# A transformer layer in one kernel: the last tiles' scales apart, more look-ahead at the end of the list, and slack behind the rounding of the feed-forward weights

## The chip, the cores and the metric

The kernel runs on one core of a Trainium2 chip. The metric is the device time of one execution in microseconds. The core has five engines that take their own instruction queues in order: PE (TensorE; its weight loads are shown as PEld), DVE (VectorE), ACT (ScalarE), POOL (GpSimd) and SP (SyncE), which here only issues transfers.

## The reference

One pre-norm transformer layer over an input of 2 sequences of 2048 tokens, 256 wide: causal attention of 16 heads of 16 with rotary positions, and a gated feed-forward layer of 704 whose activations and weights are rounded to FP4 in blocks of 16.

```python
x = x + attn(layernorm(x))           # softmax(q k^T / 4, causal) v, then Wo
x = x + ffn(layernorm(x))

def fp4_quant_dequant(x):            # blocks of 16 along the last dimension
    scale = maximum(max(abs(xb)) / 6, 1e-12)
    return GRID[searchsorted(MID, abs(xb / scale))] * sign(xb) * scale

def fp4_linear(x, w):
    return einsum('bsk,nk->bsn', fp4_quant_dequant(x), fp4_quant_dequant(w))

h = silu(fp4_linear(x, w_gate)) * fp4_linear(x, w_up)
return fp4_linear(h, w_down)
```

## The kernel before

**Work.** A sequence is four chunks of 512 tokens, a chunk four tiles of 128. The eight chunks are counted 0 to 7 here (`order`), and tile 6.3 is the last tile of chunk 6. For each chunk the kernel normalizes and projects (`norm_steps`, `project_steps`), takes the row maxima of the scores for four groups of four heads (`max_steps`; scores L1064, reduced on DVE at L1088), computes the scores again with keys on the partitions, takes exponentials on ACT and multiplies with the values (`value_steps`; L1196, L1204, L1219, L1252), divides, and runs the feed-forward layer tile by tile (`ffn_steps`). The feed-forward weights come in 18 parts (`load_rounded`): load, round, transpose on PE (L656), copy.

**A tile of the feed-forward layer.** Load `x0` and add the bias on POOL (L1472); output projection `po` (L1488), added to `x0` on DVE (L1502); statistics on DVE, the power on POOL (L520, L521); normalize (L530); round; transpose (`pth`, L1403); gate and up products in two halves each (`pg`, L1543) with DVE's L1572 and L1577; round `h`; transpose; down product `pd` (L1636, six blocks in two tasks), added on DVE (L1645) and stored (L1648). The last chunk's four tiles, 7.0 to 7.3, use space that attention has left: `own` lies in a `qT` buffer, so a load of `x0` into it has to wait until a group of heads has read its queries. They also divide by way of a transposition (L1347) and round `h` on DVE (`ON_VECTOR`); all other tiles round `h` on POOL.

**Rounding** (`fp4`): DVE finds the block scales and their reciprocals (L554 to L558), POOL shrinks the reciprocals a little (L562), POOL or DVE multiplies (L565), DVE makes a power of two of each element (L581, L584), and POOL or DVE adds and subtracts it (L587, L590) and multiplies the scale back (L593). Scale and reciprocal lie in rotating pairs of small tiles: the kinds `sc16` (256 columns) and `sc44` (704 columns).

**The list.** Nothing is issued in the order of the source. Each step becomes a task with an engine, a cost in us, a due time, and the things that it reads and writes (`Plan.add`). `Plan.ordered` plays the tasks through with the costs and writes the list: at each turn it takes, over all engines, the task that can start first; among those of one engine that could start within `PATIENCE` of each other, the one due first. For PE a change of the array's shape (64-row strips for scores, 128 by 32 for values, whole for the rest) counts `CHANGE` on the due time. It looks only at tasks due within `AHEAD` = 3 of the earliest one still open. Buffers are rooms (`ROOM`); a task that needs one waits for all users of an older thing. `late` is time that the list adds before users on other engines may start. The engines then follow the list as it is written; the chip's own waits decide when.

Due times are in units of the attention's work: a group of heads of chunk c is c + 1 units, all of it 80, so one unit is about 16 us. The last chunk's tiles are due from the end of attention on. Those of chunk 6 are spread up to four units past the end of attention (`LATE`), so that 6.3 is left over among the last tiles.

```python
horizon = dues[-1][0] + AHEAD                                   # Plan.ordered
...
return due + (CHANGE if e == PE and t.tiling != tiling else 0.0)   # rank
...
add(SP, landing(128), run, [rows_[b, c]] if last else [], [things["x0"]], due)   # ffn_steps.load
```

The last of these lines makes the load of a last tile's `x0` a reader of `rows_`, which the last division writes.

Of the kernel before, what the change touches and what calls it, by code (L numbers as in the profile page):

```python
# [29 lines left out]
F32 = mybir.dt.float32  # L30
# [8 lines left out]
P = 128  # L39
# [26 lines left out]


AHEAD = 3
CHANGE = 0.07
FEED_M = 0.0  # L70
FEED_V = 0.0
PATIENCE = 0.03
TURN = 0.3
ISSUE = 0.46

SLACK = 6.0

# [13 lines left out]
ROOM = dict(ps=7, av=1, ex=4, qT=4, parts=4)  # L91
ROOM.update(mx=2, mparts=1, left=1, mT=2, avs=1, den=2, y=2, sums=2, over=1)
ROOM.update(xnT=1, xin=XIN, high=1, t1=1, t2=1, cs=1, dev=XIN-1)
ROOM.update(x0=1, xT=1, x1=2, xn=2, h=1, hrT=1, step=1, fdev=2, sc16=2, sc44=2)


ANY_TURN = ("ps",)
# [31 lines left out]
class Plan:  # L129
# [3 lines left out]
    def __init__(self):  # L133
        self.tasks = []
        self.made = {}

    def add(
        self, engine, cost, run, reads=(), writes=(), due=0.0, books=(), tiling="whole", feeds=0.0,
# [38 lines left out]
    def ordered(self):  # L177

        waiting = {e: [] for e in HOP}
        for n, t in enumerate(self.tasks):  # L180
            if not t.left:
                waiting[t.engine].append((t.due, n, t))
        number = {t: n for n, t in enumerate(self.tasks)}
        free = dict.fromkeys(HOP, 0.0)
        rooms = {kind: [] for kind in ROOM}
        turn = dict.fromkeys(ROOM, 0)
        tiling = "whole"
        dues = sorted(((t.due, n) for n, t in enumerate(self.tasks)), reverse=True)
        done = set()
        out = []  # L190

        def vacancy(kind, n, to):

            held = rooms[kind]
            n -= ROOM[kind] - len(held)
            if n <= 0:
                return 0.0, []
            some = []
            for thing in held:
                if all(u.end is not None for u in thing.users):  # L200
                    at = max(
                        u.end + (u.late if u.engine != SP else 0.0) + HOP[u.engine][to]
                        for u in thing.users
                    )
                    some.append((at, thing.number, thing))
            if len(some) < n:
                return None
            some = sorted(some)[:n]
            return some[-1][0], [thing for *_, thing in some]

        while len(out) < len(self.tasks):
            while dues and dues[-1][1] in done:
                dues.pop()
            horizon = dues[-1][0] + AHEAD
            choice = None
            for e, queue in waiting.items():
                queue.sort(key=lambda x: x[:2])
                able = []
                vacant = {}
                for due, n, t in queue:  # L220
                    if due > horizon or len(able) > 30:
                        break
                    at = max(t.ready, free[e])
                    for kind, some in t.kinds.items():
                        if kind not in ANY_TURN and some[0].number != turn[kind]:
                            break
                        key = kind, len(some)
                        if key not in vacant:
                            vacant[key] = vacancy(*key, e)
                        if vacant[key] is None:  # L230
                            break
                        at = max(at, vacant[key][0])
                    else:
                        able.append((at, due, n, t))
                if not able:
                    continue
                first = min(at for at, *_ in able)
                if choice and first > choice[0] + 1e-9:
                    continue

                def rank(x):
                    at, due, n, t = x
                    return due + (CHANGE if e == PE and t.tiling != tiling else 0.0)

                pick = min((x for x in able if x[0] <= first + PATIENCE), key=rank)
                if choice is None or pick[0] < choice[0]:
                    choice = pick
            at, due, n, t = choice
            e = t.engine
            waiting[e].remove((due, n, t))  # L250
            for kind, some in t.kinds.items():
                for thing in vacancy(kind, len(some), e)[1]:
                    rooms[kind].remove(thing)
                rooms[kind] += some
                turn[kind] += len(some)
            if e == PE:
                if t.tiling != tiling:
                    at += ENTER[t.tiling]
                tiling = t.tiling
            if e == SP:  # L260
                free[e] = at + ISSUE * t.late
                t.end = free[e] + t.cost
            else:
                t.end = free[e] = at + t.cost
            done.add(n)
            out.append(t)
            for a in t.after:
                a.left -= 1
                late = t.late if a.engine != e and e != SP else 0.0
                a.ready = max(a.ready, t.end + late + HOP[e][a.engine])  # L270
                if not a.left:
                    waiting[a.engine].append((a.due, number[a], a))
        self.span = max(t.end for t in out)
        return out
# [29 lines left out]
def layer_kernel(  # L304
# [226 lines left out]

        add(DVE, 0.33, run, *things, due)

    def fp4(src, thing, r, n, engine=POOL, step_of=None):

        nb = n // BLOCK
        st = {}
        small16 = Thing("sc16" if nb <= 16 else "sc44")
        queue = nc.gpsimd if engine == POOL else nc.vector
        plain = on_pool(n) if engine == POOL else on_vector(n)  # L540
        by_block = 0.14 + 1.71e-3 * n if engine == POOL else on_vector(n)
# [6 lines left out]

        def scaled(due):
            def sizes():  # L550
                scale = ffn.tile([P, nb], F32, tag=f"scale{n}", name="scale")[:r]
                inv = ffn.tile([P, nb], F32, tag=f"inv{n}", name="inv")[:r]
                st["scale"], st["inv"] = scale, inv
                nc.vector.tensor_reduce(  # L554
                    scale, blocks(src()), AX.X, ALU.max, apply_absolute_value=True
                )
                nc.vector.tensor_scalar(scale, scale, 1.0 / 6.0, 1e-12, ALU.mult, ALU.max)
                nc.vector.reciprocal(inv, scale)  # L558

            def nudged():  # L560
                inv = st["inv"]
                nc.gpsimd.tensor_scalar(inv, inv, NUDGE, 1.0, ALU.mult, ALU.mult)  # L562

            def divided():
                queue.tensor_tensor(blocks(src()), blocks(src()), spread(st["inv"]), ALU.mult)  # L565

            add(DVE, on_vector(n) + 0.36 + 0.005 * nb, sizes, [thing], [small16], due)
            add(POOL, 0.17, nudged, [small16], [small16], due)
            add(engine, by_block, divided, [small16], [thing], due)

        def rounded(due):
# [24 lines left out]
            add(DVE, 0.263 + 1.033e-3 * n, powers, [thing], [step], due)  # L596
            add(engine, plain, added, [step], [thing], due)
            add(engine, plain, taken, [step], [thing], due)
            add(engine, by_block, scaled_back, [small16], [thing], due)

        return scaled, rounded

# [33 lines left out]
    def load_rounded(w, row, rows, col, cols, put, target):  # L636

        st = {}
        raw = Thing("xn")
        scaled, rounded = fp4(lambda: st["raw"], raw, rows, cols)  # L640

        def load(due):
            def run():
# [779 lines left out]
    def ffn_steps(b, c, i, last=False):  # L1423
# [33 lines left out]
        def load(due):  # L1457
            def run():
                token("x0")
                nc.sync.dma_start(st["x0"], x[b, t * P : (t + 1) * P, :])  # L1460

            add(SP, landing(128), run, [rows_[b, c]] if last else [], [things["x0"]], due)

        def turn_attended(due):
            def put():
# [43 lines left out]
        def scaled(due):  # L1509
            def dst():  # L1510
                token("xn")
                return st["xn"]

            got, dev = st["by"]
            normed(
                dst, lambda: st["x1"], got, ([dev, things["x1"]], [things["xn"]]), due
            )

            def step_of():

                things["x0"].tile = lambda: st["x0"]
                return things["x0"]

            first, st["rounded"] = fp4(
                lambda: st["xn"], things["xn"], P, E, step_of=step_of if last else None
            )
            first(due)

# [65 lines left out]
        def scaled_gated(due):  # L1594
            def step_of():
                step = Thing("ex")
                step.tile = lambda: wide("step")
                return step

            first, st["rounded"] = fp4(  # L1600
                lambda: st["hf"],
                things["h"],
                P,
                I,
                DVE if last and i in ON_VECTOR else POOL,
                step_of if last else None,
            )
            first(due)

# [253 lines left out]
    begun += [(-8.5 + 0.1 * n, step) for n, step in enumerate(both)]  # L1863
    for at, step in sorted(begun + main + side, key=lambda x: x[0]):
        step(at)
    for t in plan.ordered():
        t.run()
        in_order(t.end < DAWN)
# [62 lines left out]
```

## Time and profile before

| | |
|---|---|
| median of 3 runs | 1390.26 us (1388.22 to 1392.69) |
| the profiled execution | 1384.36 us, of which the span is 1382.6 |
| mean granted clock | 0.972 |
| PE busy | 1307.6 us (95%) |
| DVE busy | 1106.0 us (80%) |
| ACT, POOL busy | 752.0 (54%), 538.4 (39%) |

Busy time is summed over the span; a wait is idle time of an engine ahead of an instruction, put down to what ended it. In rows of the time line the columns are start, length, engine, line, operation, output and inputs with shapes, count, and in brackets the idle time before and its releaser. Groups of instructions that follow each other are merged in such rows. PE's busy time is modelled, and a PE that is busy need not be at its peak.

### The profile page before, as it was taken

The page shows a single profiled execution, that of the slowest core. Times are in us where ns is not written, and L with a number is a line of the kernel's source. Part 1 is how long each engine was busy: PE and PEld are TensorE (multiplying, and loading weights), DVE is VectorE, ACT ScalarE, POOL GpSimd, SP SyncE. Part 2 cuts the span into 40 slices and gives each one's busy share as a digit, 9 for nine tenths or more (in the row PEclk, how much of TensorE's full clock was granted, in tenths as well). Part 3 has the DMA queues.
Part 4 walks back from the last instruction along what each step waited for, and adds up shares of the span by engine and source line. Part 5 has one row for each costly group of instructions (what it writes and reads, how often), then busy time and mean ns, then how long its engine had stood idle before and what let it go on. Part 6 is the DMA issues. An engine that isn't in the chain of part 4 may idle for free.

```text
span 1382.6 us, 27442 instructions
## 1 busy us (share of the span) xinstructions
PE 1307.6 (95%) x10269; PEld 650.5 (47%) x10269; DVE 1106.0 (80%) x2415; ACT 752.0 (54%) x1670; POOL 538.4 (39%) x685
## 2 busy tenths in 40 slices
PE   6887999999999999999988999999999999999967
PEld 4444444444544444444454555454454444444445
DVE  7788989978889988875467978997879888884286
ACT  3532665556556566558643455455655566668711
POOL 4654735434323434314345544343443232311262
PEclk9976999999999999999999999999999999999989
DMA  2544433411221401211444414240130130000000
GB/s 88 132 130 103 100 89 66 102 35 55 56 46 39 109 22 35 67 32 51 98 107 108 104 30 107 65 97 18 55 82 20 43 81 9 9 6 5 13 9 19
DMA packets 61886, 84.37 MB, mean 61 GB/s; under 512 B 14772, under 2 KB 30520, under 8 KB 61752
## 3 DMA queue, kind: packets, MB, share of 16 engines
q1 hardware_dynamic: 61744, 82.61, 23.7%
q8 instruction: 81, 1.33, 0.4%
q14 instruction: 53, 0.43, 0.1%
q10 hardware_dynamic: 8, 0.00, 0.0%
HBM read 55.09 MB, written 27.49 MB: 60 GB/s over the span
## 4 chain that ended last, share of the span: by engine, by line
PE 62%; DVE 20%; POOL 5%; issue 5%; DMA 5%; ACT 2%; SPq 0%; POOLq 0%; DVEq 0%; ACTq 0%
PE av L1252 14%; DVE parts L1088 9%; PE sc L1064 9%; PE pg L1543 9%; PE sx L1196 8%; PE sx L1204 7%; PE pd L1636 5%; PE pj L808 3%; PE pth L1403 2%; PE po L1488 1%; PE pv L990 1%; DVE scale L554 1%; PE sc L1033 1%; DVE step L581 1%; DVE step L584 1%
## 5 line engine op out<-in xcount | busy, mean ns | idle before, releaser
L1219 ACT ACTIVATE ex<-sx 128x512 f32<-128x512 f32 (+3 forms) x1280 | 593.5, 538 | 345.8 <-PE sx L1204 207.9
L1088 DVE TENSOR_REDUCE parts<-sc 128x1 f32<-128x512 f32 (+3 forms) x1152 | 638.4, 611 | 64.8 <-PE sc L1064 49.2
L1204 PE MATMUL sx<-qT,kT 64*128 64x512 f32 (+3 forms) x1280 | 337.7, 523 | 0.0
L1064 PE MATMUL sc<-kT,qT 64*128 64x512 f32 (+3 forms) x1280 | 290.3, 432 | 12.5 <-DMA kT<-parts 4.2
L1252 PE MATMUL av<-ex,v 128*32 128x512 f32 (+3 forms) x2560 | 300.1, 541 | 0.0
L1196 PE MATMUL sx<-mT,less 64*128 64x512 bf16 (+3 forms) x1280 | 250.7, 356 | 9.3 <-DVE parts L1088 3.4
L1064 PEld LDWEIGHTS sc<-kT,qT 64*128 64x128 f32 x1280 | 139.1, 192 | 176.4 <-DVE parts L1088 55.2
L1196 PEld LDWEIGHTS <-less 64*128 64x128 bf16 x1280 | 68.5, 94 | 212.9 <-issue 205.4
L562 POOL TENSOR_SCALAR inv<-inv 128x16 f32<-128x16 f32 (+2 forms) x82 | 17.7, 216 | 384.8 <-DVE inv L558 362.9
L1204 PEld LDWEIGHTS sx<-qT,kT 64*128 64x128 f32 x1280 | 132.5, 196 | 13.0 <-issue 10.6
L1636 PE MATMUL pd<-wdT,hrT 128*128 128x256 f32 (+1 forms) x384 | 100.9, 402 | 2.0 <-ACT hrT L1407 1.4
L1252 PEld LDWEIGHTS av<-ex,v 128*32 128x32 f32 x2560 | 51.7, 108 | 69.8 <-issue 59.8
L860 POOL TENSOR_TENSOR t<-t,cs 128x512 f32<-128x512 f32 x31 | 39.9, 1287 | 106.7 <-DVE t L854 100.4
L1636 PEld LDWEIGHTS pd<-wdT,hrT 128*128 128x128 f32 (+1 forms) x384 | 68.1, 191 | 27.2 <-issue 13.6
L1088 DVE TENSOR_REDUCE mx<-sc 128x1 f32<-128x128 f32 (+3 forms) x128 | 54.6, 478 | 31.2 <-PE sc L1033 31.0
L808 PE MATMUL pj<-xnT,wqkT 128*128 128x512 f32 x128 | 75.3, 685 | 3.3 <-DVE v L999 1.7
L1543 PE MATMUL pg<-wgT,xT 128*128 128x352 f32 x224 | 77.3, 477 | 0.3 <-ACT xT L1407 0.2
L1543 PE MATMUL pg<-wuT,xT 128*128 128x352 f32 x224 | 74.5, 472 | 0.2
L1033 PE MATMUL sc<-pick,mask_q 64*128 64x64 bf16 x1024 | 71.8, 202 | 0.0
L587 POOL TENSOR_TENSOR h<-h,step 128x704 f32<-128x704 f32 x28 | 47.2, 1685 | 57.8 <-DVE step L584 54.5
L1033 PE MATMUL sx<-pick,mask_k 64*128 64x64 bf16 x1024 | 63.5, 197 | 0.0
L1569 ACT ACTIVATE h<-pg 128x352 f32<-128x352 f32 x64 | 29.9, 467 | 56.8 <-PE pg L1543 51.6
(156 smaller groups left out, 1522.3 us busy)
## 6 DMA issues: line engine op xcount, KB each, us to landing
qT<-parts SPq DMA_DIRECT2D x120, 128.0 KB
kT<-parts SPq DMA_DIRECT2D x120, 128.0 KB
parts<-high SPq DMA_DIRECT2D x30, 256.0 KB
parts<-t SPq DMA_DIRECT2D x30, 256.0 KB
sums<-avs SPq DMA_DIRECT2D x28, 256.0 KB
cs<-in_rope_dram SPq DMA_DIRECT2D x8, 512.0 KB
xin<-in_L_attn_x_dram SPq DMA_DIRECT2D x28, 128.0 KB
y<-sums SPq DMA_DIRECT2D x28, 128.0 KB
```

The source lines that it names most:

```text
L587: queue.tensor_tensor(src(), src(), st["step"], ALU.add)
L808: nc.tensor.matmul(got["pj"], lhsT=wqkT[:, k, i, cols], rhs=xnTs[b, c][:, k, :], start=(k == 0), stop=(k == KE - 1),)
L860: (nc.gpsimd if early and i == 0 else queue).tensor_tensor(swapped, swapped, angles[b, c][:, 1, :], ALU.mult)
L1033: nc.tensor.matmul(sc[h][:, col + at : col + at + STRIP], lhsT=strips(mask, h, half), rhs=strips(pick, h), start=False, stop=(half == 1),)
L1064: nc.tensor.matmul(sc[h][:, :cols], lhsT=strips(qT, h, d, slice(i * P, (i + 1) * P)), rhs=strips(kT, h, duo, slice(0, cols)), start=True, ...
L1088: nc.vector.tensor_reduce(dst, got[0][h][:, :cols], AX.X, ALU.max)
L1196: nc.tensor.matmul(sc[h][:, off:], lhsT=strips(less[d], h), rhs=strips(mT, h, slice(off, CH)), start=True, stop=False,)
L1204: nc.tensor.matmul(sc[h][:, off:], lhsT=strips(kT, h, duo, slice(jj, jj + P)), rhs=strips(qT, h, d, slice(off, CH)), start=False, stop=(j ...
L1219: nc.scalar.activation(st[j, d][:, h, off:], got[0][h][:, off:], AF.Exp, scale=HD**-0.5)
L1252: nc.tensor.matmul(st["av"][SLOT * s : SLOT * (s + 1), off:], lhsT=v[:, at : at + SLOT], rhs=st[j, d][:, h, off:], start=(j == 0), stop=(j ...
L1543: nc.tensor.matmul(got[half], lhsT=split("xrT")[:, k, :], rhs=wT[:, k, half * IH : (half + 1) * IH], start=(k == 0), stop=(k == KE - 1),)
L1636: nc.tensor.matmul(st["pd"], lhsT=st["hrT"][:n, k, :], rhs=wdT[:n, k, :], start=(k == 0), stop=(k == KI - 1),)
```

## The change

Five edits. (1) `CHANGE` goes from 0.07 to 0.1. (2) `NEAR`: once the earliest open task is due within eight units of the end of attention, the list looks ahead over everything (50) in place of 3. (3) The last chunk's tiles get scale and reciprocal tiles of their own, the kinds `endsc16` and `endsc44`. (4) Their loads of `x0` no longer wait for the rows of the last division and are due one unit sooner. (5) `EASE`: in the list alone, whoever uses a rounded part of the weights on another engine may start 3 us after the last step of the rounding. No instruction is added, removed or changed in size; the places of the instructions in the five queues change, from the first weight parts on, and the program gets the new small tiles.

```diff
-CHANGE = 0.07
+CHANGE = 0.1
+EASE = 3.0
+NEAR = 8.0
-ROOM.update(... sc16=2, sc44=2)
+ROOM.update(... sc16=2, sc44=2, endsc16=2, endsc44=2)
...
+        self.near_end = None
...
-            horizon = dues[-1][0] + AHEAD
+            horizon = dues[-1][0] + (AHEAD if dues[-1][0] < self.near_end else 50.0)
...
-    def fp4(src, thing, r, n, engine=POOL, step_of=None):
+    def fp4(src, thing, r, n, engine=POOL, step_of=None, end=False, weight=False):
-        small16 = Thing("sc16" if nb <= 16 else "sc44")
+        own = "end" if end else ""
+        small16 = Thing(f"{own}sc16" if nb <= 16 else f"{own}sc44")
...
-                scale = ffn.tile([P, nb], F32, tag=f"scale{n}", name="scale")[:r]
-                inv = ffn.tile([P, nb], F32, tag=f"inv{n}", name="inv")[:r]
+                scale = ffn.tile([P, nb], F32, tag=f"{own}scale{n}", name="scale")[:r]
+                inv = ffn.tile([P, nb], F32, tag=f"{own}inv{n}", name="inv")[:r]
...
-            add(engine, by_block, scaled_back, [small16], [thing], due)
+            add(engine, by_block, scaled_back, [small16], [thing], due, late=EASE * weight)
...
-        scaled, rounded = fp4(lambda: st["raw"], raw, rows, cols)
+        scaled, rounded = fp4(lambda: st["raw"], raw, rows, cols, weight=True)
...
-            add(SP, landing(128), run, [rows_[b, c]] if last else [], [things["x0"]], due)
+            add(SP, landing(128), run, [], [things["x0"]], due - 1.0 * last)
...
+    plan.near_end = end - NEAR
     for t in plan.ordered():
```

In `ffn_steps` both calls of `fp4` pass `end=last`.

More of the change, by code (lines that the diff above doesn't have):

```diff
@@ L93 @@
 ROOM.update(xnT=1, xin=XIN, high=1, t1=1, t2=1, cs=1, dev=XIN-1)
-ROOM.update(x0=1, xT=1, x1=2, xn=2, h=1, hrT=1, step=1, fdev=2, sc16=2, sc44=2)
+ROOM.update(x0=1, xT=1, x1=2, xn=2, h=1, hrT=1, step=1, fdev=2, sc16=2, sc44=2, endsc16=2, endsc44=2)
 ANY_TURN = ("ps",)
@@ L1524, in scaled @@
             first, st["rounded"] = fp4(
-                lambda: st["xn"], things["xn"], P, E, step_of=step_of if last else None
+                lambda: st["xn"], things["xn"], P, E, step_of=step_of if last else None,
+                end=last,
             )
@@ L1606, in scaled_gated @@
                 step_of if last else None,
+                last,
             )
```

## The prediction

> **What bounds the kernel now.** I read the stages first, then the long chain that ended last, then the tail engine by engine. The stage table (length, busy time and count for PE, PEld, DVE, ACT, POOL, then granted clock) has three regimes.
>
> ```profile
> 50.00:100.00 50.00, 42.38 (x388) 24.04 (x380) 35.58 (x94) 21.25 (x56) 30.92 (x44) 0.80 0.54 133
> 100.00:150.00 50.00, 42.03 (x307) 21.25 (x306) 42.88 (x100) 21.34 (x48) 25.50 (x38) 0.73 0.45 112
> ...
> 200.00:1200.00 1000.00, 975.13 (x7770) 476.00 (x7762) 829.67 (x1775) 570.16 (x1249) 381.02 (x443) 1.00 0.24 61
> 1200.00:1300.00 100.00, 99.92 (x828) 42.28 (x826) 60.38 (x121) 71.81 (x153) 20.58 (x24) 1.00 0.02 5
> 1300.00:1383.00 83.00, 63.18 (x324) 40.82 (x322) 53.75 (x110) 18.67 (x54) 29.38 (x46) 0.92 0.05 17
> ```
>
> From 200 to 1300 us PE is busy 97.5 to 99.9%: only a better fit of the list could gain there. Losses lie at the start, while the feed-forward weights are prepared, and in the tail. At the start the weights' transposes (L656) hold PE, which takes its queue in order:
>
> ```profile
> 110.41 0.51 PE L656 MATMUL ptr<-ident,wr 128*128 128x128 f32 x2 [2.22 <-POOL wr L593]
> ...
> 128.83 0.69 PE L656 MATMUL ptr<-ident,wr 128*128 128x128 f32 x2 [4.37 <-POOL wr L593]
> ```
>
> The bracket is PE's idle time ahead of the row: two of four stalls, 8.5 us together. The second has a deeper cause: POOL itself waited 12.93 us for a DVE instruction behind fourteen reductions.
>
> ```profile
> 117.95 7.93 DVE L1088 TENSOR_REDUCE parts<-sc 128x1 f32<-128x512 f32 x14 [1.97 <-PE sc L1064]
> ...
> 126.55 0.72 POOL L587 TENSOR_TENSOR wr<-wr,step 128x256 f32<-128x256 f32 x1 [12.93 <-DVE step L584]
> ```
>
> In the tail (after the last attention product, 1310 us) PE stands still while the last tiles are normalized and rounded:
>
> ```profile
> 1313.23 1.41 POOL L1472 TENSOR_TENSOR own<-own,bob 128x256 f32<-128x256 f32 x2 [17.46 <-DMA own<-in_L_attn_x_dram]
> ...
> 1325.11 0.69 PE L1403 MATMUL pth<-ident,own 128*128 128x128 f32 x2 [9.14 <-POOL own L593]
> 1326.31 4.05 PE L1543 MATMUL pg<-wgT,own 128*128 128x352 f32 x8 [0.52 <-ACT own L1407]
> 1330.20 2.53 PE L1543 MATMUL pg<-wuT,own 128*128 128x352 f32 x8
> ```
>
> and the chain ends through the leftover tile 6.3 (start, length, work):
>
> ```profile
> 1363.36 1.68 POOL h L587
> ...
> 1365.11 1.67 POOL h L590
> ...
> 1367.17 2.10 POOL h L593
> ...
> 1369.31 0.67 PE pth L1403 x4
> ...
> 1370.65 4.48 PE pd L1636 x12
> 1375.13 0.60 PE pth L1403 x4
> ...
> 1376.39 3.07 PE pd L1636 x12
> ```
>
> DVE had finished tile 7.3's rounding at 1372.98 (its last L593 started 1372.09, 0.89 long), but 7.3's transposes started at 1375.06, behind 6.3's down product.
>
> **The change, part by part.** The orders of instructions of the two programs show the moves; durations are rows of the trace.
>
> **Tail** (look-ahead, scales apart, earlier loads; they only work together). In the new order 6.3's normalized tile is rounded before attention ends, where POOL now idles for 17.46 us; its transposes and first gate half stand between the last division's transposes and 7.0's, and its other three halves right after the four output projections, in PE's 9.14 us gap. Step by step:
> - DVE is the full engine from 1333 to 1373: busy 9.79 + 20.41 + 8.43 - 0.84 = 37.8 of 40 us. Of 6.3, two L1572 and two L1577 (0.5 each), the three scale instructions (1.5) and the two of L581 and L584 (1.06) now precede that stretch: 4.6 us. They go where DVE is idle: 1310 to 1333 has 10.93 + 4.19 us of work in 23, so 7.9 free. Gain 4.6.
> - DVE's waits for POOL's L562 at the end (0.78 and 0.38, POOL busy with 6.3) go: 1.2. But for 7.1 and 7.2 scale and division now stand next to each other, with the trip over POOL between (DVE's L558 ended at 1344.86, POOL's 0.23 us began at 1344.95: about 0.35 each way through): 0.7 back. Gain 0.5.
> - 7.3's transposes no longer stand behind 6.3's down product: 1375.06 - 1372.98 = 2.1.
> - The start. The x0 loads (2.44 us in the chain, landed at 1312.3 + 2.4) come early: the new order has the first three before attention's end, the fourth after the last score, about 1306. Against that 6.3's half (1.35) and transposes (0.4) delay 7.0's own by about 1.3. The additions then run at the projections' pace instead of the loads', and POOL's rounding of 7.0 is no longer cut by 6.3's five instructions (0.2 + 0.62 + 0.73 + 0.77 + 0.62 = 2.9). Walking 7.0's chain with these rows puts its transposes at about 1323.4, not 1325.1: 1.7. The first eight gate products took 4.05 against 2.53 for the next eight; PE busy beforehand removes 1.5. As DVE's filling already uses part of this, I count half of 3.2: 1.6.
> - PE will instead be idle some 4 us before 7.3's transposes. The row nearest to that is 6.3's down product, 4.48 after 3.03 + 0.46 us of idling against 3.07 otherwise: 1.4 back.
>
> [...]
>
> Sum of the tail: 4.6 + 0.5 + 2.1 + 1.6 - 1.4 = 7.4, say 7.5. Bounds: DVE's 53.75 us of work after 1310 plus 7.5 for the last transpose, copy, product and store end at 1371 at best, 11 to gain; and 3 if only the late waits go.
>
> Moving 6.3's POOL rounding also moves collisions. In the trace DVE's L581 on 704 columns has a median of 516 ns and a maximum of 1592, DVE's L590 886 and 1639, each time beside POOL's 1.69 us instructions at 1358 to 1369. The same three POOL instructions now meet 7.0's work: I count zero net.
> [...] The trace shows the old place paying already.
>
> **Weights eased by 3 us.** In the new order the transposes behind the 2.22 and 4.37 us stalls have 6 and 10 PE tasks more ahead of them, those behind the other two (0.92, 0.99) 4 and 17, at some 0.8 us a task. If all stalls go: 8.5. But during the longest DVE was reducing without a pause, and PE's extra scores would queue for it; and some weights' rounding moves later on POOL too (the seventh from 61st to 66th place). The last weight's transpose goes from 229th to 250th of 2119 PE tasks, well ahead of the first down product at 306. Between 0 and 8.5 I take 3.
>
> **Cost of changing the array's shape, 0.07 to 0.1.** Meant to save changes of shape, but the order has 1114 of them against 1115. About half of all tasks stand at another place, mostly by one to five. PE's idle time from 200 to 1200 is 24.9 us; a different fit can add or remove some of it. I take 0, with 4 either way.
>
> Total 7.5 + 3 + 0 = 10.5 from the profiled execution's 1384.36: 1373.9, a ratio of 0.9924. The median of the runs shown is 1390.26, so 1379.7, say 1380.
>
> **The rivals.**
> - *The body gives it back (no change).* Tail 3 to 5, weights nothing, order 2 to 4 worse: 1387 to 1390. For it: half the list is moved. Against: the tail is read off directly.
> - *The stalls stay (smaller gain).* POOL's rounding moves with the transposes, PE waits 8.5 us as before: 7.5 alone, 1382.7. For it: the 12.93 us wait on DVE, which no easing mends.
> - *DVE is flooded (slower).* A larger shape cost lets strips of scores run on, DVE's reductions fall behind and PE's loads wait for PSUM. PE's weight loads already wait 55.2 us for L1088, in 90 waits. It decides once that grows by 14.7 us, 27%: then the gains are gone and 4.2 more, 1394 and above. For it: DVE is 96% busy from 400 to 500 us. Against: as many shape changes as before, so runs of one shape are no longer on average.
>
> **How the numbers follow.** Forecast (both gains) 0.55, stalls stay 0.20, no change 0.13, slower 0.12. A measurement of this kernel can tell about 0.3%, 4.2 us, from nothing; so faster 0.75, same 0.13, slower 0.12. The range reaches from both bounds (11 + 8.5 off: 1370) to no gain at all (1390).
>
> **What would show it.** Right: no L1472 waiting for the load; 6.3's L1543 rows before 7.0's; the last L593 on DVE followed at once by 7.3's transposes; 62 to 69 us from the last division's transposes (1310.0 now) to the end, where there are 72.6; PE's L656 stalls under 4 us in sum. Wrong: PE idle time from 200 to 1300 us up by more than 8 us, or DVE idle for more than 6 us after 1333.

## The result and the profile after: slower by 0.72%

The changed kernel takes 1400.34 us, the median of 5 runs (1397.06 to 1401.36); the kernel before took 1389.79 beside it (1387.15 to 1392.69). The ratio is 1.0072, 95% interval 1.0059 to 1.0084. The forecast was 1380 with a range up to 1390: sign and range were both missed. The profiled execution took 1400.52 us, its span is 1398.7.

The stage table of the changed kernel (columns as before):

```profile
50.00:100.00 50.00, 42.80 (x356) 24.91 (x358) 30.71 (x84) 20.19 (x52) 26.26 (x36) 0.73 0.50 120
100.00:150.00 50.00, 42.18 (x312) 22.36 (x312) 39.56 (x103) 18.59 (x46) 23.93 (x37) 0.73 0.46 108
200.00:1200.00 1000.00, 974.99 (x7715) 480.49 (x7714) 831.51 (x1760) 563.83 (x1239) 375.87 (x435) 0.99 0.25 62
1300.00:1399.00 99.00, 83.14 (x448) 48.19 (x446) 61.37 (x120) 34.34 (x85) 34.78 (x50) 0.93 0.03 10
```

In the middle PE is as busy as before (974.99 for 975.13, at a granted clock of 0.99 for 1.00). The first rows carry the loss: in the same 50 us DVE gets 84 instructions done for 94, busy 30.71 us for 35.58. As marks I take the copies of the attended values (`avs`), one for each group of heads. The sixth starts at 203.2 us, 189.7 before; the ninth at 328.6, 315.0 before; the last at 1325.6, 1308.5 before. Some 13 of 17 us are lost in the first 200, while the weights are prepared, and 3.5 between the ninth mark and the last. (The profiled execution of before was a quick one, 5 us under its median; the medians differ by 10.6 us.)

The stalls that EASE was to remove are gone. PE's waits from 25 to 205 us after the change (in all, times, longest) no longer show the 8.5 us for POOL at the weights' transposes, L656 before and L662 now:

```profile
PE ptm L1151 <- DVE mslots L1135: 3.9, 3, 2.4
PE sc L1070 <- DVE parts L1094: 3.8, 3, 3.3
...
PE ptr L662 <- DVE parts L1094: 0.5, 1, 0.5
```

PE now waits for DVE instead, and DVE for something new. Its waits from 20 to 330 us, before:

```profile
DVE scale L554 <- DMA wr<-in_L_ffn_w_gate_dram: 5.9, 2, 3.5
...
DVE scale L554 <- DMA wr<-in_L_ffn_w_up_dram: 1.9, 1, 1.9
```

and after:

```profile
DVE scale L560 <- DMA wr<-in_L_ffn_w_up_dram: 8.7, 2, 6.8
DVE scale L560 <- DMA wr<-in_L_ffn_w_gate_dram: 8.0, 2, 4.8
```

`wr` is the raw part of the weights; with a shorter wait that is not shown, 8.2 us of waiting for its loads became 16.8. The longest wait on DVE's time line, and SP's queue at the same time:

```profile
107.36 0.73 DVE L860 STREAM_SHUFFLE t<-qb 128x512 f32<-128x512 f32 x1
114.92 0.42 DVE L560 TENSOR_REDUCE scale<-wr 128x16 f32<-128x256 f32 x1 [6.83 <-DMA wr<-in_L_ffn_w_up_dram]
```

```profile
105.08 3.66 SPq L930 DMA_DIRECT2D kT<-parts  x8
108.85 0.83 SPq L651 DMA_DIRECT2D wr<-in_L_ffn_w_up_dram  x2
```

Read it backwards. DVE stands at its reduction because the load was issued at 108.85. It was issued then because all the parts share two buffers: a part is loaded into the buffer of the part two before it, which that part's transposes on PE set free. The seventh part's transposes ran at 105.7 us, 83.1 before; the ninth part's load, which needs that buffer, went out at 108.85 (86.85 before), behind the eight transfers of `kT`. EASE puts 3 us into each turn of this ring: from the end of the seventh part's rounding to its transposes it is 5.6 us here (from 100.1) and was 2.6 before (from 80.5). The rest of the 22 us by which the load is later had gathered ahead of that. And the reductions stand in DVE's order where the list took the load to have landed, 2.5 us after its issue; here the reduction came 6 us after it.

The tail, from the last division's transposes (1327.10) to the end, is 71.6 us for 72.6. The chain that ended last:

```profile
1386.60 0.81 DVE h L596
1387.43 0.90 DVE h L599
...
1388.38 1.13 PE pth L1409 x4
...
1390.17 5.42 PE pd L1644 x12
```

7.3's transposes now follow DVE's last step at once, and 6.3 is out of the chain. But the last product takes 5.42 us for 3.07.

### The profile page after: what moved, and what is told of

It reads as the page before. It is cut to its first block, busy times and chain, and to the rows that moved or that the text cites. A ratio compares the mean times of both kernels' runs of the same rounds, so it can differ in the third digit from the quotient of the medians.

```text
span 1398.7 us, 27458 instructions
## 1 busy us (share of the span) xinstructions
PE 1329.5 (95%) x10269; PEld 665.3 (48%) x10269; DVE 1119.1 (80%) x2415; ACT 750.4 (54%) x1670; POOL 537.4 (38%) x685
## 4 chain that ended last, share of the span: by engine, by line
PE 62%; DVE 22%; issue 5%; DMA 5%; POOL 3%; ACT 2%; SPq 0%; POOLq 0%; DVEq 0%; ACTq 0%
PE av L1258 14%; PE sc L1070 9%; DVE parts L1094 9%; PE sx L1202 8%; PE pg L1550 8%; PE sx L1210 7%; PE pd L1644 5%; PE pj L814 2%; PE pth L1409 2%; PE po L1494 2%; DVE step L587 1%; DVE scale L560 1%; DVE mx L1094 1%; PE pv L996 1%; PE sc L1039 1%
## 5 line engine op out<-in xcount | busy, mean ns | idle before, releaser
L1210 PE MATMUL sx<-qT,kT 64*128 64x512 f32 (+3 forms) x1280 | 341.9, 527 | 0.0
L1070 PE MATMUL sc<-kT,qT 64*128 64x512 f32 (+3 forms) x1280 | 293.6, 438 | 16.0 <-DVE parts L1094 5.2
L1202 PE MATMUL sx<-mT,less 64*128 64x512 bf16 (+3 forms) x1280 | 255.3, 358 | 9.5 <-DVE parts L1094 3.6
L1070 PEld LDWEIGHTS sc<-kT,qT 64*128 64x128 f32 x1280 | 142.6, 195 | 164.7 <-DVE parts L1094 52.3
L1644 PE MATMUL pd<-wdT,hrT 128*128 128x256 f32 (+1 forms) x384 | 105.1, 414 | 0.8 <-ACT hrT L1413 0.8
L1258 PEld LDWEIGHTS av<-ex,v 128*32 128x32 f32 x2560 | 52.6, 108 | 71.6 <-issue 61.8
L525 POOL TENSOR_SCALAR ve<-mv 128x1 f32<-128x1 f32 x64 | 12.6, 197 | 140.3 <-DVE mv L521 136.8
```

The lines of the kernel that those rows point to most:

```text
L1070: nc.tensor.matmul(sc[h][:, :cols], lhsT=strips(qT, h, d, slice(i * P, (i + 1) * P)), rhs=strips(kT, h, duo, slice(0, cols)), start=True, ...
L1202: nc.tensor.matmul(sc[h][:, off:], lhsT=strips(less[d], h), rhs=strips(mT, h, slice(off, CH)), start=True, stop=False,)
L1210: nc.tensor.matmul(sc[h][:, off:], lhsT=strips(kT, h, duo, slice(jj, jj + P)), rhs=strips(qT, h, d, slice(off, CH)), start=False, stop=(j ...
L1258: nc.tensor.matmul(st["av"][SLOT * s : SLOT * (s + 1), off:], lhsT=v[:, at : at + SLOT], rhs=st[j, d][:, h, off:], start=(j == 0), stop=(j ...
L1644: nc.tensor.matmul(st["pd"], lhsT=st["hrT"][:n, k, :], rhs=wdT[:n, k, :], start=(k == 0), stop=(k == KI - 1),)
```

## Experiments

DVE's idle times below are sums of the gaps ahead of its instructions from 20 to 330 us in each run's trace; "for loads" is the part ended by a load of `wr`.

| run | ratio to before, 95% | DVE idle | for loads |
|---|---|---|---|
| before | 1 | 45.2 | 8.2 |
| the change | 1.0072 (1.0059 to 1.0084) | 53.5 | 16.8 |
| change_alone | 0.9961 (0.9946 to 0.9977) | 45.3 | 7.9 |
| ease_alone | 1.0087 (1.0069 to 1.0105) | 57.4 | 16.3 |
| tail_alone | 0.9988 (0.9972 to 1.0004) | 50.2 | 8.7 |
| mid_alone | 1.0085 (1.0056 to 1.0114) | 57.4 | 18.8 |
| no_ease | 0.9943 (0.9924 to 0.9961) | 46.8 | 8.3 |
| ease_3rooms | 1.0003 (0.9992 to 1.0015) | 45.9 | 6.2 |
| plain_3rooms | 0.9996 (0.9979 to 1.0013) | 43.2 | 3.6 |
| nudged_list | 1.0026 (1.0014 to 1.0038) | 46.7 | 8.7 |
| nudged_list_2 | 1.0062 (1.0044 to 1.0079) | 53.1 | 8.1 |
| ease_late_landing | 1.0051 (1.0031 to 1.0070) | 53.1 | 0.0 |
| shape_cost_012 | 1.0034 (1.0020 to 1.0047) | 45.0 | 9.0 |
| ease_loads_early | 1.0035 (1.0017 to 1.0053) | 51.1 | 0.0 |
| after_loads_early | 1.0007 (0.9990 to 1.0024) | 46.9 | 0.0 |
| plain_loads_late | 1.0035 (1.0020 to 1.0049) | 53.4 | 13.4 |
| warm_fill | 0.9975 (0.9961 to 0.9988) | 44.6 | 7.8 |
| warm_fill_2 | 0.9926 (0.9905 to 0.9947) | 44.2 | 8.0 |

The idle times come from one execution each, the ratios from all of them, and executions of one list differ. tail_alone has before's list up to about 1190 us, and yet DVE idles 5.0 us more in it and the ninth mark comes 5.3 us later. Its waits for loads are steadier, 8.7 for 8.2.

**Which edit.** The change in its parts, each on the kernel before.

```diff
-CHANGE = 0.07
+CHANGE = 0.1        # change_alone, and with EASE mid_alone
+EASE = 3.0          # ease_alone, on the last step of a weight part's rounding
                     # tail_alone: NEAR, endsc16/endsc44, the x0 loads
```

change_alone. 

> The kernel before with one edit, CHANGE 0.07 to 0.1; the list is the same up to PE's 229th task (about 170 us). Theory A, the loss is made in the first 200 us, by an order in which the array runs at half clock for longer (the changed kernel had lost 13 us by 200 us): this edit then costs little, end of attention within 4 us of 1310, median 1387 to 1394. Theory B, the shape cost makes runs of scores that hold PE for DVE: +8 to +15 us, spread from 200 us on, median 1398 or more.

ease_alone. 

> The kernel before with one edit, EASE 3.0 on the weights' rounding. Theory A: most of the loss is here, 8 to 14 us by 200 us, longer stretches of half clock before 200 us, median 1398 to 1404. Theory B: the stalls on the weights go and nothing else, median 1384 to 1390.

tail_alone. 

> The kernel before with the three edits of the end (look-ahead, scales apart, earlier loads); the list is the same up to PE's 1908th task (about 1190 us). From the changed kernel's trace: 3.8 us earlier at the last transposes, 2.8 given back by an array at half clock behind its 3.4 us of idling. Both theories: end of attention as before within 2 us, tail 69 to 72 us against 72.6, median 1386 to 1391. My recorded sum would be 1382.

mid_alone. 

> The kernel before with CHANGE and EASE and without the three edits of the end. If the losses of the parts simply add, its time less that of the kernel before is the sum of those of the two edits alone, and end of attention is near 1327 (17 later). If the two lists are merely two draws from a wide scatter, it stands apart from the sum by 5 us or more.

EASE alone loses 0.87%, more than the whole change; CHANGE alone gains 0.39%, and with EASE in the list that gain is not to be found (mid_alone, where the two ratios multiplied would be 1.0048). change_alone, at 1385.3 us, is faster than either theory had it. The tail edits are worth 0.12%, 1.7 us, with an interval that still holds nothing; in the profile of tail_alone attention ends 7 us later than before, where both theories said within 2, and the tail is 70.0 us. Without EASE the rest should then be the better kernel.

```diff
-            add(engine, by_block, scaled_back, [small16], [thing], due, late=EASE * weight)
+            add(engine, by_block, scaled_back, [small16], [thing], due)
```

no_ease. 

> The change without EASE: CHANGE 0.1 and the edits around the end. If EASE alone makes the loss and the rest adds up, the ratio to before is 0.9961 x 0.9988 = 0.995, about 1384 us. If CHANGE's gain is luck of one list that any further edit undoes, it is 0.998 to 1.000.

It is: 1384.6 us, as the two ratios multiplied say.

**Why EASE costs.** EASE's list stands as before's ahead of PE's 36th task and behind its 436th (of 2119). I first tried a third buffer, in the list and in the tiles, with EASE and without.

```diff
-ROOM.update(... xn=2 ...)
+ROOM.update(... xn=3 ...)
-... tag="xn", name="wr", bufs=2)
+... tag="xn", name="wr", bufs=3)
```

ease_3rooms. 

> EASE alone (ratio 1.0087 with two rooms) with a third buffer for the raw weight parts, in the list and in the tiles. Theory L: the loss comes from the loads. A part is loaded into the buffer of the part two before it, which its transposes set free; EASE puts those transposes later in PE's order, so the loads stand later in SP's, and DVE's reduction of the next part stands at the head of DVE's queue until the load lands (16.3 us of such idling with EASE, 8.4 us without). With a third buffer that idling falls to 8 us or less and the time to that of the next run, within 0.3%, at or below 1391. Theory R: any other order of the first 320 us costs or gains up to a percent by the phases of the clock and the waits of in-order queues; then the third buffer has no sure effect, and EASE may still lose 0.5% or more against the next run. Theory C (the array's half clock): the loss stays at 8 to 12 us whatever the loads do, with 10 us or more of half clock above before's in the first 200 us.

plain_3rooms. 

> The kernel before with only the third buffer for the raw weight parts: the yardstick of the run before it. Theory L: DVE's idling for these loads falls from 8 us to 3 us or less, and the time by 0 to 6 us, ratio 0.996 to 1.000. Theory R: anything from 0.993 to 1.007.

The waits for loads fall from 16.3 to 6.2 us and the loss from 0.87% to nothing, within 0.3% of the same edit without EASE. That fits late loads; but the third room also moves tasks on every engine. So I asked what a list costs that is only different.

```diff
-WEIGHTS = 8
+WEIGHTS = 8.1       # nudged_list; 8.2 in nudged_list_2
```

nudged_list. 

> The kernel before with one planner constant moved that has nothing to do with the change (WEIGHTS from 8 to 8.1, a due time of the weights' parts): 390 of PE's 2119 tasks stand elsewhere, none before task 56 or after 896. Theory R: it differs from before by 0.4% or more either way, as EASE does. Theory L: it differs by what DVE idles for the loads of the weight parts more or less than before's 8 us, at 1.0 to 1.4 us of time for one of idling, and without a difference there by under 0.3%.

nudged_list_2. 

> As the nudged list (1.0026), with the constant at 8.2: a second sample of what a list costs that is only different. Theory R: beyond 0.4% either way. Theory L: within 0.4%, and DVE idles 6 to 11 us for the loads of the weight parts.

Both are slower, by 0.26 and 0.62%, with before's waits for loads. Theory L expected less than 0.4%, and the second misses that. A nudge of a list costs a few tenths of a per cent here; EASE's 0.87 is above both samples, but not so far that the rest needs no test. The other route to the same end, a longer landing in the list's costs:

```diff
-            add(SP, landing(128), run, [], [raw], due)
+            add(SP, landing(128) + 3.0, run, [], [raw], due)
```

ease_late_landing. 

> EASE alone with two rooms, but in the list's costs the load of a raw weight part takes 3 us longer (5.5 for 2.5, where the traces show 3 to 7 us from issue to the reduction), so that DVE's reduction of it is placed later in DVE's order. Theory L (the loss is DVE held at the head of its queue by a load that the list takes to have landed): DVE's idling for these loads falls from 16.3 us to 9 or less although rooms and EASE are as they were, and the time to within 0.4% of before, 1385 to 1396. Against it: EASE's later transposes cost by themselves, and the ratio stays at 1.007 to 1.011.

The waits for loads go to 0.0 and 40% of the loss goes with them, but DVE idles 53.1 us, of that now 13.6 for the loads of `den` (3.5 before), and the ratio is outside what theory L named. Undecided so far. The next three runs leave PE, DVE, ACT and POOL with the same instructions in the same order and move loads in SP's order only; the first two also have the third buffer.

```diff
+    order = plan.ordered()
+    for k in range(3, len(loads)):      # ease_loads_early, after_loads_early; SOONER = 6.0
+        at = to = order.index(loads[k])
+        first = order.index(turns[k - 3]) + 1
+        while to > first and order[to - 1].end > loads[k].end - landing(128) - SOONER:
+            to -= 1
+        order.insert(to, order.pop(at))
-... tag="xn", name="wr", bufs=2)        # and every other "xn" tile; the list keeps two rooms
+... tag="xn", name="wr", bufs=3)
...
+    for k, n in {9: 2, 10: 2}.items():  # plain_loads_late: behind the next two tasks of SP
+        at = to = order.index(loads[k])
+        while n:
+            to += 1
+            n -= order[to].engine == SP
+        order.insert(to, order.pop(at))
```

ease_loads_early. 

> EASE alone with its list kept on PE, DVE, ACT and POOL instruction for instruction; the raw weight parts get a third buffer, and their loads stand up to 6 us of the list's time earlier in SP's order. Theory L (late loads): DVE's idling for them falls from 16.3 us to 9 or less and the ratio from 1.0087 to 1.000 to 1.004. Theory R (the order of the list itself): the waits go, others take their place, and the ratio stays at 1.006 or above.

after_loads_early. 

> The whole change with the same edit of its loads and nothing else. Theory L: from 1.0072 to 0.996 to 1.001, the tail edits' 0.1 to 0.2% and the rest of EASE's loss in it. Theory R: 1.005 or above.

plain_loads_late. 

> The kernel before with two loads later in SP's order and nothing else moved on any engine: the tenth part's behind one transfer and the eight of kT that EASE's list puts ahead of it (issued at 106 in place of 99.5 us), the eleventh's behind two loads of x. Theory L: DVE meets the tenth part's reduction at about 103 us and now waits some 6 us there; of that the eleventh part's wait of 1.8 us and that for den (2.8 us) right behind may be saved, so 2 to 6 us reach the end: ratio 1.0015 to 1.0045. Theory R: no order but SP's has moved, so within 0.15%.

All three measured what theory L named, and none what theory R named. With its loads early the whole change goes from 1.0072 to 1.0007 and EASE from 1.0087 to 1.0035. Against the change without EASE (no_ease, 0.9943) the early loads give back about half of EASE's cost: 1.0072 is 1.30% above it, 1.0007 still 0.64%. Two loads put back in the kernel before cost 0.35%, 4.9 us. The DVE time line of that run shows the changed kernel's wait remade:

```profile
102.55 0.74 DVE L831 SCALAR_TENSOR_TENSOR t<-pj,bqk,cs 128x512 f32<-128x512 f32 x1
110.22 0.42 DVE L555 TENSOR_REDUCE scale<-wr 128x16 f32<-128x256 f32 x1 [6.93 <-DMA wr<-in_L_ffn_w_up_dram]
```

In the kernel before that reduction started at 101.67 without a wait. The kernel before with its own loads early was not run, so how much it would gain by them too is not known; plain_3rooms, the nearest, gained 0.04% with 3.6 us of waiting for 8.2.

With its loads early EASE has another wait, that for `den`. DVE's waits of ease_loads_early, and the longest of them on the time line:

```profile
DVE den L1333 <- DMA den<-sums: 13.6, 3, 7.0
```

```profile
107.43 0.25 DVE L1333 RECIPROCAL den<-den 128x16 f32<-128x16 f32 x1 [6.96 <-DMA den<-sums]
```

EASE alone has 6.8 us for `den` and before 3.5. SP issues this transfer no later (100.9 us, 107.3 in EASE alone), but DVE, which no raw part holds any more, stands at it from 100.5 on. So in part theory R holds: in these two traces 10 of the 16.3 us of waits that went came back as others. This trace is of an execution of 1401.3 us, where the median is 1394.1; that of after_loads_early, of 1393.0 with a median of 1391.9, has 11.8 us for `den`. That these waits make the rest of EASE's cost is not shown. Three rooms in the list itself (ease_3rooms) keep both small, 6.2 us for the loads and 7.6 for `den`.

**CHANGE.** Was its gain that of saved changes of shape?

```diff
-CHANGE = 0.07
+CHANGE = 0.12
```

shape_cost_012. 

> The kernel before with CHANGE at 0.12 alone: PE's order has 1092 changes of the array's shape, 1115 before and 1102 with CHANGE at 0.1, which measured 0.9961, that is 5.4 us for 13 changes less. If the gain is that of the changes saved, 23 less are worth up to 9.6 us, ratio 0.993; if it was the luck of one list, anything from 0.996 to 1.003.

Slower by 0.34% with the fewest shape changes. A gain by saved changes would have grown; CHANGE at 0.1 was one list among others, and a fortunate one.

**The cold products of the tail.** Fill PE's last two idle stretches, in the change without EASE.

```diff
+    def warm(t, fill, n):               # into a PSUM tile that nobody reads
+        spare = small(CH, "spare")
+        for k in range(fill):
+            j = k % (n // P)
+            nc.tensor.transpose(spare[:, (k % TPC) * P : (k % TPC + 1) * P], t[:, j * P : (j + 1) * P], ident)
...
             def powers():               # tile 7.0: 12; in warm_fill also 7.3: 16
                 ...
+                warm(t, fill, n)
             def taken():                # in warm_fill_2, 7.3: 16
+                warm(st["step"], late_fill, n)
```

warm_fill. 

> The change without EASE (1384.6 us), and PE kept busy in its last two idle stretches: 12 transposes of tile 7.0's step ahead of 7.0's transposes, 16 of tile 7.3's ahead of 7.3's, both into a spare PSUM tile that nobody reads, in PE's order at the place where the step is written. If the idling of 3.08 and 3.37 us is what makes the next products run at the half clock, the first eight gate products take 2.5 to 2.8 us for 4.01 and the last down product 3.05 to 3.3 for 4.72; the end comes 1.5 us earlier for sure and up to 3.2 if DVE follows the gate products, 1381.4 to 1383.1. If something else slows them (the copy on ACT just ahead, or PE's start after a wait), they stay at 4.0 and 4.7 and the time does not move.

The first eight gate products took 2.63 us for 4.01: right. At the end it backfired. PE's time line:

```profile
1369.44 1.97 PE L592 MATMUL spare<-ident,step 128*128 128x128 f32 x16 [1.87 <-DVE step L587]
1371.25 1.66 PE L1651 MATMUL pd<-wdT,hrT 128*128 128x256 f32 x6
```

The fill waits for 7.3's step, and the second half of 7.2's down product is queued behind it; DVE, whose next instruction adds that product, waits 2.63 us, and 7.3's last rounding steps and transposes stand behind that. The last product stays cold, behind another gap:

```profile
1375.14 1.19 PE L1415 MATMUL pth<-ident,h 128*128 128x128 f32 x6 [2.24 <-DVE h L605]
1376.58 4.22 PE L1651 MATMUL pd<-wdT,hrT 128*128 128x256 f32 x12 [0.25 <-ACT hrT L1419]
```

The kernel takes 1386.8 us, 2.2 more than without the filling.

warm_fill_2. 

> As warm_fill, but the 16 transposes of 7.3's step stand behind 7.2's last down product in PE's order, at DVE's second addition of 7.3, so that nothing of another tile waits for them. If idling makes the cold products: 7.3's transposes follow DVE within 0.3 us, the last down product takes 3.05 to 3.6 us for 4.72, and from the last division's transposes to the end it is 70.0 to 71.5 us for 73.0 in the change without EASE; ratio 0.992 to 0.996. If the cold products have another cause: 4.2 to 4.8 us, and 73.

With the fill behind that product:

```profile
1374.34 1.97 PE L541 MATMUL spare<-ident,step 128*128 128x128 f32 x16 [0.38 <-DVE step L598]
1377.33 0.87 PE L1419 MATMUL pth<-ident,h 128*128 128x128 f32 x6 [1.02 <-DVE h L609]
1378.66 3.05 PE L1655 MATMUL pd<-wdT,hrT 128*128 128x256 f32 x12 [0.46 <-ACT hrT L1423]
```

3.05 us for 4.72, and 70.9 us from the last division's transposes to the end for 73.4 (measured as the 72.6 of before). This kernel, 1381.86 us, 0.9926 (0.9905 to 0.9947), is the best measured: the change without EASE, with PE kept busy. Its interval overlaps that of no_ease (0.9924 to 0.9961), so the gain is plain in the products and not yet in the time.

## Why the prediction was wrong, step by step

**Weights eased (-3, "between 0 and 8.5"): the step that failed.** The stalls of PE went, 8.5 to 0.5 us, as read from the order. They were worth nothing, and the edit cost 12 us alone. Of the 21 us between the forecast and the measurement this step makes 15 and the tail 6; CHANGE's gain is not to be found beside EASE. Two things were wrong. The bounds began at zero, because the step followed the moved transposes on PE and their rounding on POOL, and stopped there: the buffers that the transposes free, the loads on SP that wait for those buffers, and the DVE reductions queued on those loads were not followed. And PE was taken for the engine that counts at the start, since its stalls are the plain ones to see. DVE is. In the 18 profiled executions of this study PE's idle time from 20 to 330 us lies between 25.2 and 34.1 us and hardly goes with the time (correlation 0.31; the whole change has the smallest). DVE's lies between 43.2 and 57.4, and the ninth mark comes 1.12 us later for each us of it (correlation 0.96). That is a correlation, and a late program shows less DVE work by 330 us in any case; that the waits for loads push the time is shown by plain_loads_late.

**Tail (-7.5).** Measured -1.7 (-3.9 to 0.6, tail_alone); in the profiles 72.6 became 71.6, and 70.0 in tail_alone. Term by term:
- DVE's 4.6 us of 6.3 moved ahead: mis-sized. 7.9 us of free time before 1333 were counted as room for it. DVE's idling from the last division's transposes to its last rounding step fell from 10.0 to 7.2 us only, since the moved work brings waits of its own, 1.96 us for ACT ahead of 6.3's first half. The last rounding step ends 1.8 us sooner, 61.2 us behind those transposes for 63.0.
- DVE's waits for POOL at the end, 0.5: misread. Of the 1.2 us only 0.38 was for L562; the 0.78 stood ahead of 7.2's last addition and was for its down product on PE. In the changed kernel the same kinds of wait come to 1.5 us (0.80 for a product, 0.35 and 0.34 for POOL), so nothing was gained.
- Collisions with POOL, "zero net": wrong. POOL's instructions for 6.3, and between them some for 7.3's normalized tile, now meet four of 7.0's DVE instructions, of 1.27, 1.88, 0.94 and 1.96 us where 0.89, 0.53, 0.53 and 0.89 are usual: 3.2 us, for 1.8 before. The longest two, and 6.3's on POOL beside them:

```profile
1355.36 1.88 DVE L587 TENSOR_SCALAR step<-h 128x704 int32<-128x704 int32 x1
...
1358.25 1.96 DVE L593 TENSOR_TENSOR h<-h,step 128x704 f32<-128x704 f32 x1
```

```profile
1354.53 2.33 POOL L596 TENSOR_TENSOR h<-h,step 128x704 f32<-128x704 f32 x1
...
1357.79 1.67 POOL L599 TENSOR_TENSOR h<-h,scale 128x704 f32<-128x704 f32 x1
```

 The net is 1.4 us more, not zero.
- 7.3's transposes behind 6.3's product, 2.1: right, the gap is 0.05 us.
- The start, 1.6: 7.0's transposes come 1.1 us sooner relative to the last division. But the first gate products were to run at full clock, and did not, 5.06 us for 4.05, because PE still idles 3.07 us before them; the granted clock is 0.50 from 1340.5 to 1347.3, and was 0.77 from 1326 to 1333 before.
- The cold last product, 1.4 back: 2.3 for the product and 0.5 for the transposes (the first four: 1.13 for 0.60 to 0.67), 2.8 in all. The gap ahead is 3.37 us, and the clock rows of the trace give 0.5 from 1388.3 to 1395.1. warm_fill_2 shows the cause: with 1.02 us of idling ahead the product took 3.05 us.

**CHANGE (0, 4 either way).** -5.4 us alone, and +4.7 at 0.12. The mean was fair and the bound too narrow: lists that differ in one constant ran from -5.4 to +8.6 us.

**The rivals.** "DVE is flooded" named the right sign and the right engine, with the wrong mechanism. Its point of decision, PE's weight loads waiting over 70 us for L1088, was not reached: 52.3 for 55.2. DVE was not flooded but starved. Of the signs named as wrong, one did not come: PE's idle time from 200 to 1300 us is 25.1 us for 24.9. The other, DVE idle for more than 6 us after 1333, could tell nothing: from the same place on it is 9.9 us, but the kernel before already had 8.3, most of it ahead of the last two additions. Of the signs named as right, three came. The tail is 71.6 us and not 62 to 69, and POOL still waits for two loads of `x0`, 25.1 us, though well before attention ends. Nothing on the list of signs looked at DVE before 330 us.

**The clock.** My first theory was half clock at the start. The changed kernel does lose more there (41.0 us of time times the missing share of clock before 200 us, for 29.0), but ease_late_landing loses least of all with EASE (25.6) and is still 0.5% slower. So half clock does not make EASE's loss by itself. With the loads early it is back at 29.0 in the whole change, which fits half clock following the waits; no run tests that apart.

What stays open: which of the many small moves give a nudged list its 0.3 to 0.6%, and what makes up what EASE still costs with early loads, 0.35% alone and 0.64% beside the other edits.

## What to carry to other kernels

Before a stall is priced, ask which engine paces that stretch: the idle time of an engine that does not is exchanged for another wait. When a step is put later, follow the buffer that it frees round to the load, the queue that issues the load, and the instruction that stands at the head of an in-order queue for it; here a slack of 3 us per part came back as 9 us of DVE idling. In a list scheduler any edit deals a new list, so run an unrelated nudge beside it before a difference of half a per cent is put down to the edit, and move one engine's instructions alone where you can.

## What the runs showed of the hardware

Idling of 3.07 us was enough for half clock afterwards: the clock rows of the changed kernel's trace give 0.5 from 1340.5 to 1347.3, and eight gate products took 5.06 us for 2.53. With dummy transposes that cut the idling to 0.65 us (warm_fill) the eight gate products took 2.63 us, and with 1.02 us ahead of 7.3's transposes (warm_fill_2) the last down product took 3.05. In warm_fill 2.24 us ahead of 7.3's transposes were enough: six transposes took 1.19 us and the last down product 4.22, where warm_fill_2 has 0.87 and 3.05. In no_ease gaps of 2.05 and 1.55 us with 0.44 us of transposes between them were followed by six transposes in 1.54 us and four gate products in 2.55, where the same trace has 0.88 and 1.45 later on. The changed kernel's gaps of 1.48 and 1.55 us, 0.44 us apart, were not followed by half clock: it is 1.00 from 1360 to 1372, and four gate products took 1.35 us.
